# Where a chunked scan takes up its carry: in the scan instruction or in its first decay

## The chip, the cores and the metric

One core of a Trainium2 chip runs the whole program in one launch. The metric is device time in microseconds of one execution; lower is better. The kernel before takes 10,763.39 us (median of 3 runs, 10,757.55 to 10,774.28).

The engines are called by their names: TensorE (PE in the profile; PEld is its weight load), VectorE (DVE), ScalarE (ACT), GpSimd (POOL) and SyncE (SP), which issues all the transfers of the scan phase. SBUF is the on-chip memory of 128 partitions, PSUM the memory that TensorE writes to, in banks of 128 x 512 floats.

## The reference

A block with a selective scan in four directions, a small convolution branch, then linear attention and a feed-forward part, over 8 images of 96 channels and 64 x 64 pixels. What matters here is the scan, for each of 4 directions, 192 channels d and 16 states n, along 4096 positions:

```python
def step(hst, inp):
    u_i, dt_i, b_i, c_i = inp
    dA = jnp.exp(dt_i[..., None] * A)
    hst = dA * hst + (dt_i * u_i)[..., None] * b_i[:, :, None, :]
    y = jnp.einsum('bkdn,bkn->bkd', hst, c_i)
    return (hst, y)
h0 = jnp.zeros((bb, k, d, n), u.dtype)
_, ys = lax.scan(step, h0, (u_t, dt_t, b_t, c_t))
```

So the state of every channel and every n is a running value: the decay dA times the state before it plus an input. Where a scan is cut into chunks, the last state of a chunk must enter the next one.

## The kernel before

Each image has 4 passes ("orders") over the 4096 positions, and each pass 8 chunks of 512: 32 units an image, 256 in all. A pass runs forward or backward (`u.back`). The first chunk of a pass (`u.start`) begins from state 0; there are 32 such units.

A unit has 24 slots, 6 tiles (`TILES`, n = 0 to 5) of 4 rows (m). One slot is one scan of 128 x 512: 64 channels times 2 states on the partitions, 512 positions along the row. What happens for it:

- `inputs` (L998, GpSimd): `hb` = B x (dt u) for the four rows of a tile in one instruction of 128 x 2048.
- `decays(q)` (L1123, ScalarE): the exponential of dt x A into one of four PSUM banks, tile `da`. It is issued in slot q - 2, so two slots ahead.
- The scan (L1195, VectorE, `tensor_tensor_scan`): decay times running state plus `hb`. Its start value is 0.0 in a first chunk, and otherwise `col`, a 128 x 1 column of the tile `carry` in SBUF.
- The multiplication with C. A row that is *banked* is scanned in place in its PSUM bank, and VectorE multiplies it with C into `hb` (L1201, one instruction per row, `product`, issued behind the next slot's scan); then ScalarE copies its last state into `carry` (L1202). A row that isn't banked is scanned into `hb`, and GpSimd multiplies all such rows of the tile with C in one instruction (`outputs`, L1004), in place in `hb`; before that ScalarE copies their last states into `carry` (L1207).
- `sums` (L1024, TensorE) adds up the states.

`BANKED` (L34) says how many of the four rows of each of the 6 tiles are banked: tiles 0, 2 and 4 all four, tiles 1 and 3 none, tile 5 two or three (`u.banked`, L745: three in image 0 and in all but the first pass of the other images). In numbers: 168 + 32 = 200 units with three and 56 with two.

All queues are written out by hand in program order: `plan` says which function is called in which slot of a unit, and each engine works its instructions off in that order. Beside the scans run *streams*: generators that do a small step of other work per slot (the next image's input part; the last image's gate, convolutions, attention and feed-forward). Their steps on ScalarE stand in the same queue as the exponentials, among them a silu or gelu with a table load before and behind it, which are held back to the slots 0, 1, 8, 9, 16 and 17. `step_sizes` (L971 to L980) makes the step sizes of units to come in slots 6 to 15.

In a slot ScalarE's order is: copies of carries that are due (`kept`), the exponential of the slot after next, then the slot's planned and stream work. A copy L1202 waits for the product of two slots before. An exponential waits until the bank is free, that is, until the product and the copy of the scan four before it are done. `outputs` of tile 1 is issued in slot 8, of tile 3 in slot 16, and of tile 5 in slot 0 of the next unit; it waits for the copy L1207 of its tile, since it overwrites what that copy reads. `hb` has 6 buffers.

Of the kernel before, what the change touches and what calls it, by code (L numbers as in the profile page):

```python
# [9 lines left out]
F32 = mybir.dt.float32  # L10
# [3 lines left out]
ALU = mybir.AluOpType  # L14
# [8 lines left out]
T = 512  # L23
NC = L // T
G = 4
# [5 lines left out]
SPREAD = 5  # L31
HB = 6

BANKED = ((4, 0, 4, 0, 4, 2), (4, 0, 4, 0, 4, 3))  # L34

HOLD = 3
LAND = 11
# [6 lines left out]
def kernel(ctx: ExitStack, tc: tile.TileContext, a, out):  # L44
# [8 lines left out]
    nc = tc.nc  # L53
    P = 128
# [8 lines left out]
    def bank(tag, name):  # L63
        return psum.tile([P, T], F32, tag=tag, name=name, bufs=BANKS[tag])
# [122 lines left out]
    def back_kit(pool, tag, extra, other=None, upper=0):  # L187

        k = Kit()
        k.tag, k.solo, k.upper = tag, not extra, upper  # L190
        if other is None:
            k.ya, k.za, k.bs, k.r, k.d1, k.s1, k.s2, y, z = (plain(pool, f"{tag}b{i}") for i in range(9))
            k.pad = padded(pool, tag + "pad")
        else:
            k.ya, k.za = (x.t for x in other.x)
            k.bs, k.r, k.d1, k.s1 = other.e
            k.s2, y, z = (other.pre[:, i, :] for i in range(3))
            k.pad = other.pad
        k.yb, k.zb = Part(y), Part(z[64:P])
        k.ya, k.za, k.bs = Part(k.ya), Part(k.za), Part(k.bs)  # L200
        if pool is None:
            return k
        k.t2 = Part(k.r), k.ya
        k.ln = Part(pool.tile([C + 1, T], F32, name=tag + "ln"))
        nc.gpsimd.memset(k.ln.t, 1.0)
        k.im = other.im if other else Part(pool.tile([C + 1, 18, W2], F32, name=tag + "im"))
        k.m3 = [Part(pool.tile([C, 8, W2], F32, name=f"{tag}m3{i}")) for i in range(2)]
        k.gm = gm0 if not extra else pool.tile([P, 8, W2], F32, name=tag + "gm")
        if extra:
            nc.gpsimd.memset(k.gm, 0.0)  # L210
        k.x8 = pool.tile([C, T], F8, name=tag + "x8")
        k.h16 = pool.tile([P, 3, T], F16, name=tag + "h16")
        k.h8 = pool.tile([P, 3, T], F8, name=tag + "h8")
        k.o16 = pool.tile([C, T], F16, name=tag + "o16")
        return k
# [479 lines left out]
    def in_turn(stages, k, settle):  # L695

        for stage, cs in stages:
            yield from stage(k, cs)
            if settle:
                yield from settled()  # L700
# [12 lines left out]
    def drained(*streams, beside=()):  # L713
        while any(s.on for s in streams):
            tick()
            for s in (*streams, *beside):
                s.run()

    def all_issued():
        drained(Stream(iter((HOLD + 1,))))  # L720
# [12 lines left out]
    units, images = [], []  # L733
    for b in range(out.shape[0]):

        s = {"b": b, "done": set(), "live": b + 1 == out.shape[0], "pairs": (1, 0) if b else (0, 1)}
        images.append(s)
        for order, (pair, back) in enumerate((p, k) for p in s["pairs"] for k in range(2)):
            for i in range(NC):
                u = Unit()  # L740
                u.s, u.pair, u.back, u.k = s, pair, back, pair + 2 * back
                u.c, u.start = (NC - 1 - i if back else i), i == 0
                u.order, u.new, u.i = order, (order, i) == (0, 0), len(units)
                u.bc, u.hb, u.delta, u.du, u.p = {}, {}, {}, {}, {}
                u.banked = BANKED[int(b == 0 or u.i % 32 >= NC)]  # L745
                units.append(u)

    TILES = [(g, j) for g in range(2) for j in range(3)]
# [3 lines left out]
    first = front(0, images[0])  # L752
# [170 lines left out]
    sp = scan_pool.enter_context(tc.tile_pool(name="scan", bufs=2))  # L923
# [76 lines left out]
    def outputs(u, n):  # L1000

        lo = u.banked[n]
        hb = u.hb[n][:, lo:, :]
        nc.gpsimd.tensor_tensor(hb, hb, u.bc[1, TILES[n][0]][:, lo:, :], ALU.mult)  # L1004

# [51 lines left out]
    def plan(u, last, nxt, third, fourth):  # L1057
# [6 lines left out]
        if last:  # L1064
            put(0, outputs, last, 5)
            for m in range(2):
                put(m, sums, last, (3, 4), 2 + m)
            for m in range(2):
                put(3 + m, sums, last, (5,), m)
            put(3, gather, last, 0)  # L1070
            put(7, states, u, 1, 1)
            put(7, gather, last, 1)
# [4 lines left out]
        if third and u.i % 2:  # L1077
            put(16, step_sizes, (nxt, third), 5)
        put(8, outputs, u, 1)
        put(16, outputs, u, 3)  # L1080
        for m in range(4):
            put(13 + m, sums, u, (0, 1), m)
# [30 lines left out]
    def at_index(i):  # L1113
        return units[i] if 0 <= i < len(units) else None

    def decays(q):

        if q >= 24 * len(units):
            return
        u, (n, m) = units[q // 24], divmod(q % 24, G)  # L1120
        g, j = TILES[n]
        da[q] = bank("da", "da")
        nc.scalar.activation(  # L1123
            da[q], u.delta[j], AF.Exp, scale=a_neg[:, u.k, j, g * G + m : g * G + m + 1]
        )

    da, kept, side, carry, product = {}, [], [], None, None
    for u in units[:2]:
        fetched_dt(u)
    fetched_u(units[0])  # L1130
# [10 lines left out]
    inputs(units[0], 0)  # L1141
    inputs(units[0], 1)
    decays(0)
    decays(1)
    for i in range(6):
        step_sizes(units[1:2], i)

    def advance(n):

        tick()  # L1150
        for st in side[:]:
            st.run()

    for u in units:
        last, nxt, third, fourth = (at_index(u.i + d) for d in (-1, 1, 2, 3))
        if u.new:
            drained(*side)
            b = u.s["b"]
            side = []
            if b == 0:  # L1160
                half_done.pace = 1.0
                side += [Stream(behind(kit_2, pairs[3:])), half_done]
            else:
                side.append(Stream(chain((SETTLE,), in_turn(back_end(b - 1, last.s), kit_b, False))))
            if b == 0:
                pass
            elif b + 1 < out.shape[0]:
                side.append(Stream(in_turn(front(b + 1, images[b + 1]), kit_f, True), PACE))
            else:
                final = back_end(b, u.s)  # L1170
                last_kit = back_kit(None, "f0", True, kit_f)
                side.append(Stream(final[0][0](last_kit, range(1, NC)[::-1])))
        if u.i == pairs[2] - 2:
            drained(half_done, beside=side[:1])
            side[1] = Stream(in_turn(front(1, images[1]), kit_f, True), PACE * (1 - u.i / 32))
        if u.i == pairs[3] - 2:
            drained(side[0])
        if fourth and fourth.new:
            drained(*side[-1:])
            all_issued()  # L1180
        if u.start:
            carry = sp.tile([P, 24], F32, tag="carry", name="carry")
        todo = plan(u, last, nxt, third, fourth)
        for slot in range(24):
            n, m = divmod(slot, G)
            g, j = TILES[n]
            q, hb, first_at = 24 * u.i + slot, u.hb[n], 0 if u.back else T - 1
            col = carry[:, 8 * j + g * G + m : 8 * j + g * G + m + 1]
            while kept:
                kept.pop(0)()  # L1190
            decays(q + 2)
            d = da.pop(q)
            banked = m < u.banked[n]
            dd, x = (d[:, ::-1], hb[:, m, ::-1]) if u.back else (d, hb[:, m, :])
            nc.vector.tensor_tensor_scan(dd if banked else x, dd, x, 0.0 if u.start else col, ALU.mult, ALU.add)  # L1195
            if product:
                product()
                product = None
            if banked:
                def product(d=d, x=hb[:, m, :], c=u.bc[1, g][:, m, :], col=col, at=first_at):  # L1200
                    nc.vector.tensor_tensor(x, d, c, ALU.mult)  # L1201
                    kept.append(lambda: nc.scalar.copy(col, d[:, at : at + 1]))  # L1202
            elif m == G - 1:
                lo = 8 * j + g * G
                kept.append(
                    lambda c=carry[:, lo + u.banked[n] : lo + G].unsqueeze(2), h=hb[:, u.banked[n] :, :], at=first_at:
                    nc.scalar.copy(c, h[:, :, at : at + 1])  # L1207
                )
            for f, args in todo[slot]:
                f(*args)  # L1210
            place[0] = slot
            advance(slot)
    place[0] = None
    if product:
        product()
# [87 lines left out]
```

## Time and profile before

| | us |
|---|---|
| median of 3 runs | 10,763.4 |
| the profiled execution | 10,764.7 |
| its span, first to last instruction | 10,763.0 |
| from the first scan's start to the last scan's end | 10,351.6 (from 181.0 to 10,532.6) |
| VectorE busy in the span | 10,158.1 (94%) |
| GpSimd busy | 10,118.0 (94%) |
| TensorE busy | 8,423.7 (78%) |
| ScalarE busy | 7,397.8 (69%) |
| DMA queue q1, share of the time of 16 engines | 84.5% |

In 38 of the 40 slices of the span VectorE and GpSimd are at 90% or more; the first and the last slice hold the preparation and the last image's end. The granted clock of TensorE is 0.841 on the mean.

The largest groups of instructions, beside those that the next part shows:

```profile
L998 POOL TENSOR_TENSOR hb<-b,du 128x2048 f32<-128x2048 f32 x1536 | 6952.6, 4546 | 6.1 <-DMA du<-ua 5.2 <-PE p L1024 0.9
L1123 ACT ACTIVATE da<-delta,w_a_logs 128x512 f32<-128x512 f32 x6144 | 4164.3, 689 | 541.5 <-DVE hb L1195 447.5 <-DMA delta<-nat 5.2
L1004 POOL TENSOR_TENSOR hb<-hb,c 128x2048 f32<-128x2048 f32 x512 | 2323.8, 4539 | 197.7 <-ACT carry L1207 180.1 <-DMA c<-xd 13.2 <-DMA y<-yt 4.4
L1202 ACT COPY carry<-da 128x1 f32<-128x1 f32 x3784 | 593.8, 157 | 2054.5 <-DVE hb L1201 2045.1
```

Such a row gives the line, the engine, the operation, what it writes and reads by the program's names, the shapes and the count; behind the first bar busy microseconds of the group and mean nanoseconds of one; behind the second the idle time of the engine just before these instructions and what ended most of it.

### The profile page before, as it was taken

The numbers are of one execution on the slowest core, as the hardware profiler recorded it, in microseconds if no ns is written. First come the engines' busy times: TensorE is split into PE (matmuls) and PEld (weight loads), VectorE is DVE, ScalarE is ACT, GpSimd is POOL, SyncE is SP. The second block draws the span as 40 slices with busy tenths as digits, with TensorE's granted clock in tenths as the row PEclk, the third lists the DMA queues.
The fourth block names the chain that finished last, engine by engine and source line by source line (L and its number), as shares of the span: only waits on it lengthen the run. The fifth ranks groups of instructions, "written<-read, shape, count | busy, mean of one in ns | idle before, by whom it ended". The sixth has DMA issues, their size and how long they took to land. (4 is left out here: it accounts for less than half of the span.)

```text
span 10763.0 us, 97608 instructions
## 1 busy us (share of the span) xinstructions
PE 8423.7 (78%) x23270; PEld 2274.2 (21%) x23270; DVE 10158.1 (94%) x11126; ACT 7397.8 (69%) x15154; POOL 10118.0 (94%) x2782
## 2 busy tenths in 40 slices
PE   7777668886788867888688886888768887677677
PEld 2121112221122211222122221222112221111112
DVE  3999999999999999999999999999999999999993
ACT  4666666777676776777767776677766767666674
POOL 3999999999999999999999999999999999999991
PEclk8888788987889878998789887898778987778788
DMA  6888888998889988898888988889888898888883
GB/s 148 208 205 209 200 209 214 226 226 200 215 216 227 227 193 220 216 231 219 201 218 214 237 212 202 217 220 237 198 211 218 219 235 200 202 203 210 208 214 94
DMA packets 1095381, 2253.29 MB, mean 209 GB/s; under 512 B 435993, under 2 KB 436698, under 8 KB 963731
## 3 DMA queue, kind: packets, MB, share of 16 engines
q1 hardware_dynamic: 1094803, 2247.05, 84.5%
q8 instruction: 184, 3.01, 0.1%
q14 instruction: 394, 3.23, 0.1%
HBM read 1507.14 MB, written 336.69 MB: 171 GB/s over the span
## 5 line engine op out<-in xcount | busy, mean ns | idle before, releaser
L998 POOL TENSOR_TENSOR hb<-b,du 128x2048 f32<-128x2048 f32 x1536 | 6952.6, 4546 | 6.1 <-DMA du<-ua 5.2
L1024 PE MATMUL p<-hb,halves 128*64 128x512 f32 x12288 | 3713.8, 707 | 1053.0 <-POOL hb L1004 562.6
L1123 ACT ACTIVATE da<-delta,w_a_logs 128x512 f32<-128x512 f32 x6144 | 4164.3, 689 | 541.5 <-DVE hb L1195 447.5
L1195 DVE TENSOR_TENSOR_SCAN da<-da,carry,hb 128x512 f32<-128x512 f32 x3311 | 4164.0, 1274 | 90.7 <-ACT carry L1202 37.0
L1004 POOL TENSOR_TENSOR hb<-hb,c 128x2048 f32<-128x2048 f32 (+2 forms) x768 | 2714.3, 3534 | 222.3 <-ACT carry L1207 203.0
L1195 DVE TENSOR_TENSOR_SCAN hb<-da,carry,hb 128x512 f32<-128x512 f32 x2065 | 2547.0, 1265 | 1.8
L1201 DVE TENSOR_TENSOR hb<-da,c 128x512 f32<-128x512 f32 x3784 | 2534.0, 670 | 1.8 <-DMA c<-xd 0.9
L1202 ACT COPY carry<-da 128x1 f32<-128x1 f32 x3784 | 593.8, 157 | 2054.5 <-DVE hb L1201 2045.1
L1024 PEld LDWEIGHTS p<-hb,halves 128*64 128x64 f32 x12288 | 904.8, 157 | 3697.8 <-issue 1876.0
L313 PE MATMUL conv<-f0im,taps 97*128 97x512 f32 (+1 forms) x2088 | 867.7, 655 | 37.2 <-ACT f0pre L369 32.2
L1195 DVE TENSOR_TENSOR_SCAN da<-da,hb 128x512 f32<-128x512 f32 x473 | 566.1, 1214 | 28.0 <-POOL hb L998 26.6
L963 PE MATMUL dt<-dts,dt_w 7*128 7x512 f32 (+1 forms) x1024 | 485.9, 742 | 92.3 <-ACT carry L1207 36.2
L980 POOL TENSOR_TENSOR ua<-nat,ua 128x512 f32<-128x512 f32 x256 | 329.9, 1289 | 170.9 <-DVE nat L977 161.8
L313 PEld LDWEIGHTS conv<-f0im,taps 97*128 97x128 f32 (+1 forms) x2088 | 256.4, 173 | 588.2 <-issue 508.8
L1207 ACT COPY carry<-hb 128x4 f32<-128x4 f32 (+2 forms) x768 | 149.7, 195 | 302.1 <-DVE hb L1195 293.7
L1195 DVE TENSOR_TENSOR_SCAN hb<-da,hb 128x512 f32<-128x512 f32 x295 | 346.8, 1205 | 1.7 <-ACT carry L1202 1.7
L259 PE MATMUL var<-f1e,ones_c 96*96 96x512 f32 x350 | 225.6, 731 | 121.8 <-ACT f1e L256 68.5
L253 PE MATMUL ctr<-f1e,cen_c 96*96 96x512 f32 x402 | 218.1, 649 | 86.1 <-ACT f1e L592 34.2
L977 DVE SCALAR_TENSOR_TENSOR nat<-dt,nat 128x512 f32<-128x512 f32 x384 | 258.0, 672 | 17.9 <-ACT nat L975 12.7
L975 ACT ACTIVATE nat<-nat,one 128x512 f32<-128x512 f32 x384 | 271.8, 708 | 0.1
L497 PE MATMUL cab<-f1im,cab_w 97*32 97x512 f32 x1044 | 256.0, 603 | 12.5 <-DMA f1im<-xld 7.1
L275 ACT ACT_TABLE_LOAD x193 | 247.6, 1283 | 4.1 <-PEq L1292 0.8
(430 smaller groups left out, 7586.0 us busy)
## 6 DMA issues: line engine op xcount, KB each, us to landing
b<-xd SPq DMA_DIRECT2D x1024, 512.0 KB
c<-xd SPq DMA_DIRECT2D x1024, 512.0 KB
delta<-nat SPq DMA_DIRECT2D x1536, 128.0 KB
du<-ua SPq DMA_DIRECT2D x1024, 128.0 KB
y<-yt SPq DMA_DIRECT2D x512, 256.0 KB
u<-y SPq DMA_DIRECT2D x384, 256.0 KB
ua<-u SPq DMA_DIRECT2D x256, 256.0 KB
du<-ub SPq DMA_DIRECT2D x512, 128.0 KB
```

Source lines behind the costliest of these rows:

```text
L313: nc.tensor.matmul(ps, taps[:, t, lo : lo + n], im[:, r0 + dy : r0 + dy + 8, dx : dx + HW], start=t == 0, stop=t == 8,)
L963: nc.tensor.matmul(ps, dt_w.rearrange("r j d -> r (j d)")[32 * w.k : 32 * w.k + R + 1, d], w.dts, start=True, stop=True)
L975: nc.scalar.activation(u.nat, u.nat, AF.Ln, bias=one)
L977: nc.vector.scalar_tensor_tensor(u.nat, u.ps, 0.0, u.nat, ALU.max, ALU.add)
L980: nc.gpsimd.tensor_tensor(x, u.nat, x, ALU.mult)
L998: nc.gpsimd.tensor_tensor(hb, u.bc[0, g], u.du[j].unsqueeze(1).to_broadcast([P, G, T]), ALU.mult)
L1004: nc.gpsimd.tensor_tensor(hb, hb, u.bc[1, TILES[n][0]][:, lo:, :], ALU.mult)
L1024: nc.tensor.matmul(ps, halves, u.hb[n][:, i, :], start=TILES[n][0] == 0 and m == 0, stop=False, skip_group_check=True)
L1123: nc.scalar.activation(da[q], u.delta[j], AF.Exp, scale=a_neg[:, u.k, j, g * G + m : g * G + m + 1])
L1195: nc.vector.tensor_tensor_scan(dd if banked else x, dd, x, 0.0 if u.start else col, ALU.mult, ALU.add)
L1201: nc.vector.tensor_tensor(x, d, c, ALU.mult)
L1202: kept.append(lambda: nc.scalar.copy(col, d[:, at : at + 1]))
```

## The change

The start value of a scan is now a constant. In a unit that isn't a first chunk, `decays` lets ScalarE multiply the first decay of the chunk (column 0, or the last column in a backward pass) by the carry, in place in the PSUM bank, and the scan starts from 1.0 instead of `col`. First chunks start from 0.0, as before, and get no multiplication. The carry tile is now kept at the unit (`u.carry`), since `decays` works two slots ahead, across the border of units. That is 224 x 24 = 5376 more instructions on ScalarE, and the copies of the carries stay, as far as their rows are banked as before.

Besides, `BANKED` has one row more in the last tile: three instead of two, and four instead of three, the latter only in even units; odd ones that had three keep three. Where all four rows of tile 5 are banked, `outputs` has nothing to do and returns, and the copy L1207 of that tile isn't made. In numbers: 100 units with four, 156 with three, so 3940 banked rows where there were 3784.

```diff
-BANKED = ((4, 0, 4, 0, 4, 2), (4, 0, 4, 0, 4, 3))
+BANKED = ((4, 0, 4, 0, 4, 3), (4, 0, 4, 0, 4, 4))
...
-                u.banked = BANKED[int(b == 0 or u.i % 32 >= NC)]
+                u.banked = BANKED[int((b == 0 or u.i % 32 >= NC) and u.i % 2 == 0)]
...
         lo = u.banked[n]
+        if lo == G:
+            return
...
             da[q], u.delta[j], AF.Exp, scale=a_neg[:, u.k, j, g * G + m : g * G + m + 1]
         )
+        if not u.start:
+            u.carry = units[u.i - 1].carry
+            first = da[q][:, T - 1 : T] if u.back else da[q][:, 0:1]
+            nc.scalar.mul(first, first, state(u.carry, j, g, m))
+
+    def state(carry, j, g, m, n=1):
+        return carry[:, 8 * j + g * G + m : 8 * j + g * G + m + n]
...
         if u.start:
-            carry = sp.tile([P, 24], F32, tag="carry", name="carry")
+            u.carry = sp.tile([P, 24], F32, tag="carry", name="carry")
...
-            nc.vector.tensor_tensor_scan(dd if banked else x, dd, x, 0.0 if u.start else col, ALU.mult, ALU.add)
+            nc.vector.tensor_tensor_scan(dd if banked else x, dd, x, 0.0 if u.start else 1.0, ALU.mult, ALU.add)
...
-                def product(d=d, x=hb[:, m, :], c=u.bc[1, g][:, m, :], col=col, at=first_at):
+                def product(d=d, x=hb[:, m, :], c=u.bc[1, g][:, m, :], col=state(u.carry, j, g, m), at=first_at):
...
-                    lambda c=carry[:, lo + u.banked[n] : lo + G].unsqueeze(2), h=hb[:, u.banked[n] :, :], at=first_at:
+                    lambda c=state(u.carry, j, g, lo, G - lo).unsqueeze(2), h=hb[:, lo:, :], at=first_at:
```

In the changed file the exponential stands at L1125, the new multiplication at L1131, the scan at L1203, the product at L1209, the copies at L1210 and L1215, and `outputs` at L1006.

More of the change, by code (lines that the diff above doesn't have):

```diff
@@ L1125, in decays @@
         )
-    da, kept, side, carry, product = {}, [], [], None, None
+        if not u.start:
[4 more added lines that the diff above has]
+        return carry[:, 8 * j + g * G + m : 8 * j + g * G + m + n]
+    da, kept, side, product = {}, [], [], None
     for u in units[:2]:
@@ L1187 @@
             q, hb, first_at = 24 * u.i + slot, u.hb[n], 0 if u.back else T - 1
-            col = carry[:, 8 * j + g * G + m : 8 * j + g * G + m + 1]
             while kept:
@@ L1203 @@
             elif m == G - 1:
-                lo = 8 * j + g * G
+                lo = u.banked[n]
                 kept.append(
-                    lambda c=carry[:, lo + u.banked[n] : lo + G].unsqueeze(2), h=hb[:, u.banked[n] :, :], at=first_at:
+                    lambda c=state(u.carry, j, g, lo, G - lo).unsqueeze(2), h=hb[:, lo:, :], at=first_at:
                     nc.scalar.copy(c, h[:, :, at : at + 1])
```

## The prediction

> **What bounds the kernel now.** First the totals per engine and the groups of instructions by shape (busy us, mean ns of one | idle before them).
>
> ```profile
> PE 8423.7 (78%) x23270; PEld 2274.2 (21%) x23270; DVE 10158.1 (94%) x11126; ACT 7397.8 (69%) x15154; POOL 10118.0 (94%) x2782
> ...
> L1195 DVE TENSOR_TENSOR_SCAN da<-da,carry,hb 128x512 f32<-128x512 f32 x3311 | 4164.0, 1274 | 90.7 <-ACT carry L1202 37.0 <-POOL hb L998 36.2 <-ACT da L1123 15.7
> L1195 DVE TENSOR_TENSOR_SCAN hb<-da,carry,hb 128x512 f32<-128x512 f32 x2065 | 2547.0, 1265 | 1.8
> L1201 DVE TENSOR_TENSOR hb<-da,c 128x512 f32<-128x512 f32 x3784 | 2534.0, 670 | 1.8 <-DMA c<-xd 0.9
> L1195 DVE TENSOR_TENSOR_SCAN da<-da,hb 128x512 f32<-128x512 f32 x473 | 566.1, 1214 | 28.0 <-POOL hb L998 26.6 <-ACT da L1123 1.2
> L1004 POOL TENSOR_TENSOR hb<-hb,c 128x512 f32<-128x512 f32 x200 | 258.2, 1291 | 20.4 <-ACT carry L1207 18.9 <-DMA du<-ua 0.6 <-DMA f1x<-td 0.6
> L1195 DVE TENSOR_TENSOR_SCAN hb<-da,hb 128x512 f32<-128x512 f32 x295 | 346.8, 1205 | 1.7 <-ACT carry L1202 1.7
> L1004 POOL TENSOR_TENSOR hb<-hb,c 128x1024 f32<-128x1024 f32 x56 | 132.3, 2362 | 4.2 <-ACT carry L1207 4.0
> ```
>
> VectorE and GpSimd are both the bound. The scans run from 181 to 10,533 us, 40.4 us for each of the 256 units; in it VectorE is busy 39.4 us and GpSimd 39.4 us, and each waits about 1 us, in part for the other. A gain must come on both. What is to be seen in the scan rows: the 768 scans of first chunks, which start from 0.0, take 60 ns less than the 5376 that read a carry, in both forms. It is no overlap: from the start of one scan to the next instruction the timeline has 1.19 us with a carry and 1.13 without. Then the waits, in total and in times:
>
> ```profile
> ACT carry L1202 <- DVE hb L1201: 2045.1, 2297, 6.1
> ...
> POOL hb L1004 <- ACT carry L1207: 203.0, 159, 7.9
> ...
> DVE da L1195 <- POOL hb L998: 62.9, 67, 6.9
> ...
> DVE f1x L450 <- ACT f1e L449: 56.3, 33, 4.2
> ...
> DVE da L1195 <- ACT carry L1202: 37.0, 19, 3.2
> ...
> DVE da L1195 <- ACT da L1123: 16.8, 35, 1.9
> ```
>
> ScalarE follows VectorE in step: it idles 2045 us at the copies of carries until a product with C is done. VectorE waits little for ScalarE, some 175 us in all lines of the scan phase, half of it at L450. This spare time of ScalarE is what the change spends.
>
> **VectorE's own work.** 3311 x (1274 - 1214) + 2065 x (1265 - 1205) ns = 323 us less. Against it: of the 200 units with three banked rows in the last tile, the 100 even ones get a fourth, and the 56 with two get a third: 156 more products. One takes 670 ns, but the timeline has 0.59 us to the next start: 156 x 0.59 = 92 us more. Net -231 us.
>
> **GpSimd's own work.** The last tile's multiplication with C now costs 258.2 + 132.3 = 390.5 us; afterwards 156 single rows at 1291 ns, 201 us. Net -189 us. Its other rows stay.
>
> **ScalarE's work.** Each of the 5376 exponentials behind a first chunk is followed by a one-column multiplication in place, in PSUM, with a column of SBUF as its scale, which waits for the exponential itself. No row has this; bounds from both sides:
>
> ```profile
> 5034.02 0.69 ACT L1123 ACTIVATE da<-delta,w_a_logs 128x512 f32<-128x512 f32 x1 [0.35 <-DVE hb L1195]
> 5034.65 0.63 ACT L246 ACTIVATE var<-var,eps 96x512 f32<-96x512 f32 x1
> 5035.31 0.57 ACT L247 ACTIVATE var<-var 96x512 f32<-96x512 f32 x1
> 5035.81 0.68 ACT L1123 ACTIVATE da<-delta,w_a_logs 128x512 f32<-128x512 f32 x1
> ```
>
> Columns are start, length, instruction. L247 works in place on what L246 wrote and starts 0.03 us after its end; L246, independent, started 0.06 before the end of the one ahead. So the dependence costs 0.09 us. The length: a copy of one column (L1202) takes 0.159 us and a copy of 512 columns of PSUM (L1049) 0.578, thus 0.82 ns a column; L246 without 511 columns is 0.216 us, the exponential without them 0.270. The gate's one-column exponential with a pointer has 0.244:
>
> ```profile
> L568 ACT ACTIVATE gate<-ca,w_ca_b x8: 244/244/257, 2121.6 to 10647.9; 96x1 f32<-96x1 f32 x8
> ```
>
> I take 0.216, since L246 too reads and writes PSUM with one pointer. Behind it the next one overlaps by 0.06 to 0.10, say 0.08. ScalarE's queue thus grows by 0.09 + 0.22 - 0.08 = 0.23 us per exponential; ends: 0.09 + 0.159 - 0.10 = 0.15 and 0.09 + 0.27 = 0.36. In total 1240 us, 8630 of some 10,660: 81% on the mean. The 156 further copies of carries and 100 fewer of L1207 are some 10 us.
>
> On VectorE such a multiplication of one column takes 150 ns (L554): 806 us for 5376 of them on an engine that has no room, while ScalarE idles; so where it is put I take as right. Against this stands the Trainium skill, "ScalarE: Activation LUTs", section Rules for kernel authors, which wants multiplications on VectorE. The same page's section What ACT_TABLE_LOAD costs gives an instruction 186 ns, 93 more for a pointer operand, and 93 of overlap; from that I estimate a growth of 0.28, stalls of some 195 us and a time of 10,727.
>
> **What of it lies on the path.** An exponential is issued two slots ahead of its scan, so the queue may fall behind by a margin. I paired the 6144 exponentials with the scans and took the time from the end of the one to the start of the other: under 0.3 us in 108, under 0.6 in 307, under 1.0 in 717, under 2.0 in 2232 cases. Then a tally down ScalarE's rows: behind each exponential of a later chunk the lag rises by 0.23 us plus 0.04 that VectorE's slots become shorter (231 / 6144); each idle stretch of ScalarE takes its length off; where the lag exceeds the margin of what VectorE reads next (the scans, L450 behind L449, L977 behind L975, the products with L247's result), the difference is a stall and leaves the lag. It gives 135 us in some 300 places, 74 of it before scans, 26 at L450. With 0.15 + 0.04: 73 us; with 0.36 + 0.04: 325 us. Most falls where a table load, a silu and a second load stand in the queue, as in these four slots (us; DVE, ACT and POOL are the third to fifth busy columns):
>
> ```profile
> 5785.10:5791.90 6.80, 3.69 (x18) 0.79 (x14) 6.61 (x9) 6.50 (x11) 6.80 (x2) 1.00 1.01 252
> ```
>
> ScalarE has 6.50 of 6.80 us there, and 4 x 0.23 = 0.92 more doesn't fit; what is late next is the scan, and behind it the products, then GpSimd's L1004, which waits for the copy L1207.
>
> **Sum.** VectorE: -231 + 135 = -96 us. GpSimd: -189 us, so VectorE's sum decides. The profiled execution took 10,764.7 us (span 10,763.0, 1.7 around it), 1.3 above the median of 10,763.4: 10,763 - 96 = 10,667, said as 10,665. Its own range goes from 10,576, no stall and GpSimd's 189, to 10,763 - 231 + 265 = 10,797 at a growth of 0.33.
>
> **Rivals.**
> *ScalarE has room enough* (0.17). The stalls vanish in waits that exist anyway, since in the order-3 units, which run at 40.0 us with no idle GpSimd, VectorE is not the bound. GpSimd's term decides: 10,575. For: the 2045 us of idle; against: the 108 margins under 0.3 us.
> *ScalarE becomes the bound* (0.20), the slower side. Place: the slots around a silu, a gelu or L971 to L975, where ScalarE is full already. The stalls cost more than VectorE gains once they exceed 231 us, at a rise of about 0.345, thus a growth of 0.31 per exponential; with 0.36 it is 325 us: 10,763 + 94 = 10,857. For: 0.31 lies inside my bounds. Against: both rows nearest to the multiplication in place and size (0.216, 0.244) stay under 0.28 with overlap.
> *The change doesn't do what it says* (0.02): the 60 ns of first chunks don't come from the constant. Then 92 + 135 us come on top: 10,990. Against: the same 60 ns in both forms, and at the one place where the timeline passes from the one to the other.
>
> **How the numbers follow.** The forecast has 0.61; 0.08 of that ends within 0.2% of the time before (21 us, what a measurement of this kernel can tell from no change) and 0.02 above. Faster: 0.51 + 0.17 = 0.68; same: 0.08 and 0.02 of the second rival, 0.10; slower: 0.02 + 0.18 + 0.02 = 0.22. The range, 10,570 to 10,800, holds the forecast's own and the room rival, and leaves out the heavier part of the slower one.
>
> **What would show it.** Right: scans at L1203 near 1214 and 1205 ns in all rows; 3940 products; single-row L1006 156 times; the multiplication at 0.20 to 0.25 us; ScalarE's busy share near 80%; VectorE's idle before scans put down to the multiplied da, some 75 us more than now. Wrong: a multiplication over 0.3 us or a wait of its own over 0.1; idle time of ScalarE at the copies of carries under 600 us; slower GpSimd rows.

## The result and the profile after

The changed kernel takes 10,825.65 us (median of 4 runs, 10,816.12 to 10,829.2) against 10,760.47 in the same session: ratio 1.0058, 95% interval 1.0043 to 1.0073. It is slower by 0.6%, 65 us, where 95 us less were forecast. The profiled execution has a span of 10,814.4 us, 51 more than before.

The totals per engine and the rows by shape that answer to those of before:

```profile
PE 8463.4 (78%) x23270; PEld 2288.7 (21%) x23270; DVE 9961.1 (92%) x11282; ACT 8584.2 (79%) x20586; POOL 9940.7 (92%) x2682
...
L1203 DVE TENSOR_TENSOR_SCAN da<-da,hb 128x512 f32<-128x512 f32 x3940 | 4735.3, 1215 | 223.7 <-ACT da L1131 76.7 <-POOL hb L998 67.2 <-ACT carry L1210 66.4
...
L1209 DVE TENSOR_TENSOR hb<-da,c 128x512 f32<-128x512 f32 x3940 | 2641.8, 671 | 2.2 <-DMA c<-xd 1.3
L1203 DVE TENSOR_TENSOR_SCAN hb<-da,hb 128x512 f32<-128x512 f32 x2204 | 2586.5, 1206 | 33.7 <-ACT da L1131 21.5 <-ACT carry L1210 10.1
L1006 POOL TENSOR_TENSOR hb<-hb,c 128x2048 f32<-128x2048 f32 x512 | 2319.9, 4531 | 398.7 <-ACT carry L1215 387.9 <-DMA c<-xd 10.8
L1131 ACT ACTIVATE da<-da,carry 128x1 f32<-128x1 f32 x5376 | 1269.5, 236 | 174.5
...
L1210 ACT COPY carry<-da 128x1 f32<-128x1 f32 x3940 | 626.7, 159 | 1069.8 <-DVE hb L1209 1054.9
```

The change does to the work what it says: every scan now takes 1215 or 1206 ns, VectorE is busy 197 us less and GpSimd 177. Yet both are at 92% where they were at 94%: the work that left them came back as idle time, and more. What is waited for (total us, times, longest):

```profile
DVE da L1203 <- ACT da L1131: 76.7, 93, 3.4
DVE da L1203 <- POOL hb L998: 67.2, 68, 6.9
DVE da L1203 <- ACT carry L1210: 66.4, 28, 3.5
DVE f1ln L597 <- ACT var L247: 65.8, 28, 19.4
DVE f1x L450 <- ACT f1e L449: 59.9, 45, 5.0
...
DVE f1x L653 <- ACT var L247: 36.7, 31, 5.4
```

```profile
POOL hb L1006 <- ACT carry L1215: 422.8, 201, 6.7
```

VectorE waits for ScalarE before scans and also before the streams' instructions (L597, L450, L653); GpSimd's wait for the copy of carries has doubled from 203 us. Added up over VectorE's instructions from the first scan of unit 3 to that of unit 253 ("idle in the scan phase" from here on), its idle time was 255 us and is 497. So -197 + 242 = +45, which is the span's 51 but for the ends.

A stretch of ScalarE's timeline (start, length, instruction) shows the price of one multiplication:

```profile
5778.09 0.69 ACT L1125 ACTIVATE da<-delta,w_a_logs 128x512 f32<-128x512 f32 x1
5778.81 0.24 ACT L1131 ACTIVATE da<-da,carry 128x1 f32<-128x1 f32 x1
5778.97 0.16 ACT L1210 COPY carry<-da 128x1 f32<-128x1 f32 x1
5779.17 0.69 ACT L1125 ACTIVATE da<-delta,w_a_logs 128x512 f32<-128x512 f32 x1
```

The multiplication starts 0.03 us after the end of its exponential, and what follows starts 0.08 us before its own end: 0.72 + 0.16 = 0.88 us from one instruction to the next, where an exponential alone took 0.63 (the first two lines of the prediction's timeline). The queue grows by 0.25 us each time.

### The profile page after: what moved, and what is told of

Its sections match the earlier page's. It is cut to its first block, busy times and chain, and to the rows that moved or that the text cites. A ratio compares the mean times of both kernels' runs of the same rounds, so it can differ in the third digit from the quotient of the medians.

```text
span 10814.4 us, 103121 instructions
## 1 busy us (share of the span) xinstructions
PE 8463.4 (78%) x23270; PEld 2288.7 (21%) x23270; DVE 9961.1 (92%) x11282; ACT 8584.2 (79%) x20586; POOL 9940.7 (92%) x2682
## 5 line engine op out<-in xcount | busy, mean ns | idle before, releaser
L998 POOL TENSOR_TENSOR hb<-b,du 128x2048 f32<-128x2048 f32 x1536 | 6942.2, 4540 | 6.3 <-DMA du<-ua 5.2
L1203 DVE TENSOR_TENSOR_SCAN da<-da,hb 128x512 f32<-128x512 f32 x3940 | 4735.3, 1215 | 223.7 <-ACT da L1131 76.7
L1125 ACT ACTIVATE da<-delta,w_a_logs 128x512 f32<-128x512 f32 x6144 | 4237.3, 691 | 458.1 <-DVE hb L1203 356.9
L1006 POOL TENSOR_TENSOR hb<-hb,c 128x2048 f32<-128x2048 f32 (+1 forms) x668 | 2519.8, 3772 | 435.6 <-ACT carry L1215 422.8
L1209 DVE TENSOR_TENSOR hb<-da,c 128x512 f32<-128x512 f32 x3940 | 2641.8, 671 | 2.2 <-DMA c<-xd 1.3
L1203 DVE TENSOR_TENSOR_SCAN hb<-da,hb 128x512 f32<-128x512 f32 x2204 | 2586.5, 1206 | 33.7 <-ACT da L1131 21.5
L1210 ACT COPY carry<-da 128x1 f32<-128x1 f32 x3940 | 626.7, 159 | 1069.8 <-DVE hb L1209 1054.9
L1131 ACT ACTIVATE da<-da,carry 128x1 f32<-128x1 f32 x5376 | 1269.5, 236 | 174.5
L534 PE MATMUL cab<-f1m,cab_w 96*96 96x512 f32 x348 | 224.5, 772 | 48.7 <-ACT f1e L543 26.2
L971 ACT ACTIVATE nat<-dt 128x512 f32<-128x512 f32 x384 | 227.9, 593 | 27.7 <-PE dt L963 20.4
```

Source lines behind the costliest of these rows:

```text
L998: nc.gpsimd.tensor_tensor(hb, u.bc[0, g], u.du[j].unsqueeze(1).to_broadcast([P, G, T]), ALU.mult)
L1125: nc.scalar.activation(da[q], u.delta[j], AF.Exp, scale=a_neg[:, u.k, j, g * G + m : g * G + m + 1])
L1131: nc.scalar.mul(first, first, state(u.carry, j, g, m))
```

## The experiments

All times are medians; the ratio is to the kernel before, in the same session. The idle time is that of the one profiled execution of each run.

| run | time, us | ratio (95%) | VectorE idle in the scan phase, us |
|---|---|---|---|
| kernel before | 10,760 to 10,767 | | 255 |
| changed kernel | 10,826 | 1.0058 (1.0043 to 1.0073) | 497 |
| start and multiplication, old rows | 10,789 | 1.0022 (1.0013 to 1.0032) | 560 |
| rows only | 10,812 | 1.0041 (1.0026 to 1.0056) | 211 |
| no multiplication | 10,621 | 0.9863 (0.9847 to 0.9880) | 335 |
| multiplication by one | 10,919 | 1.0141 (1.0126 to 1.0156) | 393 |
| no multiplication, old rows | 10,626 | 0.9871 (0.9856 to 0.9885) | 417 |
| even units only, old rows | 10,754 | 0.9988 (0.9979 to 0.9998) | 371 |
| multiplication last | 10,729 | 0.9965 (0.9952 to 0.9977) | 450 |
| multiplication last, old rows | 10,725 | 0.9962 (0.9947 to 0.9976) | 512 |
| split place, old rows | 10,730 | 0.9967 (0.9954 to 0.9980) | 509 |
| six slots from the carry, old rows | 10,710 | 0.9945 (0.9929 to 0.9962) | 420 |
| by one, last | 10,880 | 1.0104 (1.0089 to 1.0119) | 362 |
| fourteen or eighteen slots, old rows | 10,678 | 0.9917 (0.9903 to 0.9930) | 364 |

### The two halves of the change

Start and multiplication, with the banked rows of before:

```diff
-BANKED = ((4, 0, 4, 0, 4, 3), (4, 0, 4, 0, 4, 4))
+BANKED = ((4, 0, 4, 0, 4, 2), (4, 0, 4, 0, 4, 3))
...
-                u.banked = BANKED[int((b == 0 or u.i % 32 >= NC) and u.i % 2 == 0)]
+                u.banked = BANKED[int(b == 0 or u.i % 32 >= NC)]
```

> Only the first half of the change: the scans start from 1.0 and ScalarE multiplies each later chunk's first decay by its carry, but the banked rows are those of the kernel before. Theory 'queue' (the 5376 multiplications make ScalarE's queue late, and VectorE and GpSimd wait for it): VectorE's own work falls by some 290 us and its waits grow by some 240 as in the changed kernel, GpSimd's own work stays, so 10,770 to 10,830 us. Rival 'rows' (the 156 further products and their alternation between units cost what the scans save): faster than before, bounded by GpSimd's unchanged work, 10,700 to 10,750 us.

10,789 us: in the range of "queue", outside that of "rows". The scans' saving is lost without any of the further rows. VectorE's own work fell by 289 us, as expected, but its waits grew by 305, more than the 240 expected. Next the rows alone, the kernel before with the changed `BANKED`:

> Only the second half: the scans take the carry as in the kernel before, the last tile has the changed kernel's banked rows. VectorE's own work grows by 91 us and GpSimd's falls by 189. Theory 'queue': VectorE is the bound, 10,800 to 10,860 us, and VectorE's waits do not grow. Rival 'rows': the same or more, with VectorE's waits for ScalarE or GpSimd grown by 100 us or more.

10,812 us, 47 more, with VectorE's idle time smaller than before (211 us). As "queue" had it: VectorE is the bound, and 90 us of work added to it is a loss. GpSimd's saving of 177 us turned into waiting, its wait for the copy doubling from 203 us with only 32 us of work added to ScalarE:

```profile
POOL hb L1006 <- ACT carry L1209: 416.9, 208, 7.9
...
ACT carry L1209 <- DVE hb L1197: 273.5, 242, 5.4
```

So the doubled wait in the changed kernel is no mark of a late ScalarE by itself; here the copy in its turn waits for VectorE's scan (L1197).

### ScalarE's load alone

The changed kernel without the multiplication; it leaves the carries out:

```diff
-            first = da[q][:, T - 1 : T] if u.back else da[q][:, 0:1]
-            nc.scalar.mul(first, first, state(u.carry, j, g, m))
```

> The changed kernel without the 5376 multiplications on ScalarE; the carries are left out of the result, all else stays. Theory 'queue': VectorE's waits fall back to some 250 us in the scan phase and both engines keep their smaller work, 10,540 to 10,610 us. Rival 'rows': above 10,750 us.

10,621 us, 144 less than before: the multiplications, where they stand, cost the changed kernel 205 us, and without them it is faster. But the gain is below the range I gave, and that matters for the prediction:

```profile
PE 8367.9 (79%) x23270; PEld 2261.5 (21%) x23270; DVE 9938.5 (94%) x11282; ACT 7413.9 (70%) x15210; POOL 9935.4 (94%) x2682
```

```profile
DVE da L1201 <- POOL hb L998: 90.0, 99, 7.4
...
DVE da L1201 <- ACT carry L1208: 42.0, 25, 3.2
...
DVE da L1201 <- ACT da L1125: 37.9, 40, 2.4
```

VectorE's work is 220 us less, but 80 us of it came back as idle time with no load added anywhere: scans reach ScalarE's exponentials (16.8 us before) and GpSimd's `hb` (62.9) earlier and wait longer. The reverse, the kernel before with the load alone:

```diff
             da[q], u.delta[j], AF.Exp, scale=a_neg[:, u.k, j, g * G + m : g * G + m + 1]
         )
+        if not u.start:
+            first = da[q][:, T - 1 : T] if u.back else da[q][:, 0:1]
+            nc.scalar.mul(first, first, one)
```

> The kernel before, with 5376 multiplications of the first decay by a column of ones at the place where the changed kernel multiplies by the carry; the scans still start from the carry. Only ScalarE's load is changed. Theory 'queue': the whole price of the multiplications shows, VectorE's waits grow by 200 us or more, 10,900 to 11,000 us. Rival 'rows': within 0.3% of the kernel before.

10,919 us, 154 more, in the range of "queue"; VectorE's idle time grows by 137 us, less than the 200 expected, but with nothing changed on VectorE itself.

Another cause would be TensorE's granted clock, which was 0.832 in the changed kernel and 0.841 before. The runs speak against it: five executions of the run "multiplication last" took 10,715 to 10,733 us at 0.835 to 0.838, those of "multiplication by one" 10,912 to 10,922 at 0.833 to 0.836. And of VectorE's idle time in the scan phase (pauses over 0.15 us), 41 us are put down to waits for TensorE in the changed kernel and 24 before.

### The scans' saving alone

The run without multiplications, with the banked rows of before; it leaves the carries out too.

> The scans start from 1.0, no multiplication on ScalarE (the carries are left out of the result), and the banked rows of the kernel before: the scans' own saving of some 300 us alone. If VectorE is the bound throughout, the 91 us of further products that are gone come on top of what the run without multiplications gained: 10,530 us. If GpSimd, whose own work is back at the old amount, takes over as the bound: 10,650 to 10,720.

10,626 us, the same as with the new rows, and in neither range. The 304 us saved on VectorE give 137. What took the rest:

```profile
PE 8408.4 (79%) x23270; PEld 2294.6 (22%) x23270; DVE 9854.0 (93%) x11126; ACT 7380.9 (69%) x15154; POOL 10114.1 (95%) x2782
```

```profile
DVE da L1201 <- POOL hb L998: 178.2, 139, 7.0
```

VectorE now waits 178 us for GpSimd, before 63. Without ScalarE's load the two engines are so close that the rows move the bound from the one to the other and change nothing in the end.

### Where the multiplications are dear

Only even units multiply; odd ones start from the carry, with the old rows:

```diff
+            if u.i % 2 == 0:
+                first = da[q][:, T - 1 : T] if u.back else da[q][:, 0:1]
+                nc.scalar.mul(first, first, state(u.carry, j, g, m))
...
-            nc.vector.tensor_tensor_scan(dd if banked else x, dd, x, 0.0 if u.start else 1.0, ALU.mult, ALU.add)
+            nc.vector.tensor_tensor_scan(dd if banked else x, dd, x, 0.0 if u.start else state(units[u.i - 1].carry, j, g, m) if u.i % 2 else 1.0, ALU.mult, ALU.add)
```

> Banked rows of the kernel before; only the even units multiply by the carry and start from 1.0, odd ones start from the carry as before (ScalarE is busy 26.8 us in an even unit of the kernel before and 29.7 in an odd one). Half of the scans' saving, some 150 us. Theory 'queue': the price rises with what the queue holds already, so the even units cost well under half, 10,660 to 10,740 us. Rival 'each multiplication has its fixed price': half of what the run with all of them and the old rows showed, 10,765 to 10,790.

10,754 us, between the two ranges: better than a fixed price for each, by far not the gain that "queue" gave. Then the place in the queue, with the changed kernel's rows: `decays` doesn't multiply any more, `carried` does, and is called at the end of the slot:

```diff
-            nc.scalar.mul(first, first, state(u.carry, j, g, m))
...
             place[0] = slot
             advance(slot)
+            carried(q + 2)
```

> The changed kernel with each multiplication issued at the end of its slot, behind the slot's other work on ScalarE, instead of right behind its exponential; where other work stands between, the wait of the multiplication for the exponential goes away, some 0.09 us. Theory 'queue' in the form that the occupied time counts: 10,750 to 10,800 us. Rival 'lateness of the decay': the multiplication is now behind the stream's instructions, the scans wait more, 10,830 to 10,900.

10,729 us, 97 less than the changed kernel, and faster than the kernel before; more than the 10,750 to 10,800 expected in this direction. In 2874 of the 5376 cases no other work stands in between and the multiplication still follows its exponential directly; in the others its own wait is gone (where it followed without a pause, it started 0.10 us before the end of the instruction ahead, on the mean of 2454). The streams' instructions also come earlier. The waits (of an execution of 10,755 us, the longest of its six):

```profile
DVE da L1209 <- ACT da L1137: 200.4, 111, 3.7
DVE da L1209 <- POOL hb L998: 74.2, 66, 6.9
...
DVE f1ln L597 <- ACT var L247: 49.8, 9, 18.4
DVE f1x L450 <- ACT f1e L449: 44.5, 34, 4.3
...
DVE hb L1209 <- ACT da L1137: 40.0, 79, 2.9
...
DVE f1x L653 <- ACT var L247: 18.5, 17, 5.4
```

The scans wait more for the multiplied decay (240 us in place of 98), as the rival said, but they no longer wait for a copy (77 in the changed kernel), and L597, L450 and L653 wait less. How much comes from the shorter time in the queue and how much from the streams' being first, no run here separates. With the old rows:

> The same place of the multiplications with the banked rows of the kernel before. Theory 'queue': 10,720 to 10,770 us. Rival 'lateness of the decay': 10,790 to 10,860.

10,725 us, in the range of "queue"; the rows make no difference in this form.

The six slots around a silu or gelu, with the multiplication right behind its exponential there, and last in the others:

```diff
             decays(q + 2)
+            if slot in CALM:
+                carried(q + 2)
...
-            carried(q + 2)
+            if slot not in CALM:
+                carried(q + 2)
```

> As the run with the multiplications last and the old rows, but in the six slots where a silu or gelu with its table loads may stand (0, 1, 8, 9, 16, 17) the multiplication is issued right behind its exponential again. In that run some 150 of the 230 us of waits before scans stand at the slots 2, 3, 10, 18 and 19, whose exponentials are issued there. Theory 'lateness': the multiplication behind 4 us of table loads and silu is late, and the split takes 60 to 100 us away: 10,630 to 10,680 us. Rival 'full queue': ScalarE has no room in these slots wherever the multiplication stands, and the waits go to the streams' own instructions: 10,710 to 10,740.

10,730 us, in the range of the rival "full queue", though only in part by its account. Of the 232 us of waits for ScalarE before scans, of which 173 stood at slots 18, 19, 3 and 10, 202 are left, 138 of them now at 20, 19, 4 and 9; the waits for ScalarE before other instructions, to which the rival wanted them to go, grew by 15 us, and VectorE's idle time is the same (509 us for 512). Where ScalarE has 4 us of table loads and silu, this other order of the rest was of no help. So no multiplication in these slots; their scans start from the carry:

> Multiplications last, old rows, but the scans whose exponentials are issued in those six slots start from the carry and have no multiplication: a quarter of the scans' saving, some 80 us, is given up, and a quarter of ScalarE's further load with it. If these slots carry most of the price (over 80 us of waits): 10,650 to 10,715 us. If the price is spread evenly: 10,730 to 10,760.

10,710 us: though 81 us of the scans' saving are given up, it is 15 us faster, in the range given for a price that stands in these slots above all; for an even one it was 10,730 to 10,760.

> The kernel before with 5376 multiplications by one, now at the end of each slot: the price of the multiplications alone at that place, beside the 154 us that they cost right behind their exponentials. Theory 'queue', in which the place sets the price: 40 to 100 us, 10,800 to 10,865. Rival 'the place helps only together with the shorter scans': 10,890 to 10,930.

10,880 us, 113 more than before, in neither range. The place at the end takes 41 us off the price of 154, not half of it or more; beside the shorter scans it took 64 (old rows) and 97 off.

The last one drops four more slots of odd units, where the run with six slots less still showed waits:

```diff
+    def starts_at_one(q):
+        i, slot = divmod(q, 24)
+        return (slot - 2) % 24 not in CALM and not (i % 2 and slot in (14, 15, 20, 21))
```

> As the run that starts the scans of six slots from the carry; in odd units four more slots (14, 15, 20 and 21) do so, where that run still shows some 80 us of waits before scans, 31 of which the kernel before has too. Given up: 4 x 112 scans at 60 ns, 27 us. If these waits come from the multiplications, 45 of them go: 10,685 to 10,700 us. If they are put off to later scans: 10,715 to 10,740.

10,678 us, ratio 0.9917 (0.9903 to 0.9930), a little better than expected, though what is given up is 31 us (4 x 128 scans; all odd units count). It has 3520 multiplications instead of 5376 and beats both kernels.

```profile
PE 8356.7 (78%) x23270; PEld 2274.1 (21%) x23270; DVE 9964.0 (93%) x11126; ACT 8025.7 (75%) x18674; POOL 10118.1 (95%) x2782
```

```profile
DVE da L1213 <- POOL hb L998: 121.3, 98, 7.4
...
DVE da L1213 <- ACT da L1141: 10.9, 29, 1.4
...
DVE hb L1213 <- ACT da L1141: 6.1, 18, 0.6
```

VectorE does as much as in the changed kernel, but its scans wait only 17 us for multiplied decays (10.9, and 6.1 of the scans into `hb`), where they waited 98 there and 226 with the multiplications last and the old rows.

## Why the prediction was wrong

**The bound.** Right: two engines side by side, and a gain must come on both. The sum then didn't keep to it.

**VectorE's own work, -231.** Measured -197. The scans gave 305 us instead of 323, the products took 91 as forecast, and the rest of VectorE's lines 17 more; an instruction behind a wait doesn't overlap with the one ahead of it. In the trace before, VectorE's instructions that follow without a pause overlap by 0.083 us on the mean; its pauses between the first and the last scan, short ones too, rose from 449 to 692, which by that overlap is an estimated 20 of the missing 34 us.

**GpSimd's own work, -189.** Measured -177.

**ScalarE's queue, +0.23 us per exponential.** Measured 0.25; the multiplication takes 236 ns, not 216. The bounds held, and 236 lies between the two nearest rows (216 and 244 ns). The estimate from the Trainium skill, "ScalarE: Activation LUTs", section What ACT_TABLE_LOAD costs, was 280 ns before overlap; the measurement is 44 ns below it. Its time, 10,727, was too low as well: the price of the instruction wasn't the main error. The same tally on the trace before, at the measured 0.25, gives 157 us and not 135. With the measured own work the sum is then -197 + 157 = -40, still a gain. The page's rule that multiplications belong on VectorE wasn't tried here.

**The step that failed** is the sum "VectorE: -231 + 135 = -96 us", by its second term. The waits grew by 242 us. By place and releaser (pauses over 0.15 us), those for ScalarE grew by 119 before scans, where the tally had 74, and by 83 before other instructions, where it had 61; those for TensorE, GpSimd and the rest, which it left out, by 37. The runs split the 242 us by cause: 80 us come from the shorter work alone (no multiplication), 162 from the multiplications on top. For the first, the tally only let the shorter slots raise ScalarE's lag by 0.04 us each, which is 34 of its 135 us (it gives 101 without). Otherwise the saving was taken as arriving whole. In fact 220 us less work on VectorE gave 144 us of time even with ScalarE's load left out, and 304 us less gave 137 with GpSimd's work left as it was: VectorE came sooner to the waits for GpSimd's `hb` and for ScalarE's exponentials and copies, and these had no term. For the second, the tally's 101 us became 137 on the kernel before (the tally at 0.25 gives 117), and 162 once the slots were shorter. The sum of the misses: 80 - 34, 162 - 101 and 34 of own work are the 141 us between -96 and +45.

**"So VectorE's sum decides".** Right for the rows, which I counted but whose sign I didn't draw out: 92 us onto the engine that decides. Alone they cost 47 us, in the changed kernel some 37 (10,826 and 10,789 us), with no multiplication nothing.

**The rivals.** "ScalarE becomes the bound" is the nearest to what came: the stalls cost more than VectorE gained. But its condition, a growth of 0.31 us, wasn't met: 0.25 was enough, because part of the gain was gone already. Its place fits the runs: once the six slots around the table loads and four slots of odd units had no multiplication, 17 of 226 us of waits for multiplied decays were left. "ScalarE has room enough" is refuted by the 154 us of multiplications by one, "the change doesn't do what it says" by the scan rows.

**The marks.** The scans, the products, the multiplication and ScalarE's 79% came as said; the idle time before scans put down to the multiplied decay grew by 81 us (17 to 98), near the 75. But the scans' waits for copies of carries, which the mark left out, grew by 38 beside it (39 to 77). None of the three marks of being wrong came either: the multiplication took 0.236 us with a wait of 0.03, ScalarE's idle time at the copies of carries was 1055 us, and GpSimd's rows weren't slower. They watched prices, and what failed was the sum of the waits.

## What to carry to other kernels

Here two engines were busy to within 1% of each other, and 304 us saved on one alone were worth 137. So count what the faster engine will then wait for before adding anything. An engine at 69% isn't free: its idle time stands in some places of its queue and not in others. Here small work did better at the end of a slot, and better still left out where the queue was full: the best of these runs pays up to 0.25 us on ScalarE for 60 ns on VectorE in 3520 places of 5376.

## What the runs showed of the hardware

On ScalarE an instruction that depends on the one just ahead started 0.03 us after its end (L247 behind L246, L1131 behind L1125); independent ones started 0.06 to 0.10 us before it. So of the 0.25 us that a multiplication right behind its exponential costs, some 0.1 is the dependence, an estimate from these rows. VectorE's scan took 60 ns more with a start value read from SBUF (1274 and 1265 ns) than with a constant, 0.0 (1214 and 1205) or nearly all 1.0 (1215 and 1206). GpSimd's L998 took 4539 to 4559 ns in the runs whose scans all start from a constant, and 4539 to 4546 in those where they take the carry.
